# A two-level Winograd kernel: who makes the opening's block sums, where GpSimd waits, and the order of A12's products

## The chip, the cores and the metric

One NeuronCore of a Trainium2 chip. The metric is the device time of one execution in microseconds; a kernel's time is the median of its runs.

## The reference

With x of 1024 x 512, 64 weight matrices W_e of 512 x 512, and a linear layer with weights of 512 x 512 and a bias, all in float32:

```
out_lin     = x @ lin_w.T + lin_b
xv          = einsum('bf,efm->bem', x, weight)
zp          = einsum('bf,efm->bem', square(x), square(weight))
interaction = 0.5 * sum(square(xv) - zp, axis=1)
return out_lin + interaction
```

The sum over e of zp is one product, square(x) times the sum of the squared weights. What costs time is xv: 64 products of 1024 x 512 by 512 x 512.

## The kernel before, in words

**Tiling.** Four weight matrices side by side make one right-hand matrix B of 512 x 2048; 16 such groups ("quarters", q = 0 to 15) make up the 64. A is x. A times B is computed with Winograd's form of Strassen's method, on two levels, so that 7 x 7 = 49 block products stand in for 64. Each block product contracts over 128, has 256 rows (two halves j of 128) and 512 columns. Its left operand is a block sum of x, held in SBUF in `xs[:, outer, inner]`; its right operand is a block sum of the weights.

Blocks and sums are named by digits, on both levels alike. For x: "1" is A11, "2" is A12, "4" is A22, and "5" = A21 + A22, "6" = "5" - A11, "7" = A11 - A21, "3" = A12 - "6". A21 itself is not an operand. `outer_x(i)` (L154) makes the outer sum i in two instructions, one of 128x768 and one of 128x256. `inner_x(i)` (L178) makes the four inner sums of outer block i, in the order 5, 6, 7, 3 (L181 to L184), each 128x256. `a21_a22_sums` (L240, the sums themselves at L252) makes the inner sums of A21 and A22, which the linear layer needs. `xs` is made once, in the opening, and used by all quarters.

For the weights GpSimd makes the sums in every quarter: `outer_t` (L382) the outer ones, in place in the weight buffers or in T5 and T6, and `inner_t` the inner ones, `tp` (128x1024, L393), `t6` and `t4` (128x512, L395 and L397).

**A unit.** `unit(q, i, j)` is one outer product i and row half j: seven inner products on TensorE (L423) in the order 1, 5, 6, 2, 7, 3, 4 into three PSUM banks x, v and y. ScalarE copies x to y after product 1 (L477). VectorE adds the banks to earlier results in SBUF (L448 to L469), with ScalarE helping in unit 1. In a quarter the outer products come in the order 1, 2, 6, 7, 5, 3, 4. In unit 5 GpSimd also adds two halves of z with `rest` (L474). Results z are squared by ScalarE and added to `acc` by DMAs with accumulation that GpSimd issues (`gather`, L508). The squared weights are summed in `w2_sum` in the same way (L517 on ScalarE, L524 the DMA).

**The linear layer** stands ahead of quarter 0. `lin` (L204) multiplies A11 plainly (L214), ScalarE puts twice the result into acc (L224). A12's products are seven inner products of `lin_p` (L272, r = 0), those of A21 and A22 seven double ones (r = 1), into the banks x_lin, v_lin and y_lin. VectorE's `lin_add` (L315) and ScalarE's `twice` (L304) put the banks into acc or into the scratch s_lin. Each product that comes back to a bank has to wait until the last reader of that bank is through.

**What sets the order.** Nothing is scheduled by a planner: each step is put into a list with `st.at(t, fn)`, sorted by t, and issued in this order, and each engine keeps its own order. One unit of t is about one product; quarter q begins at 98 q. So the numbers t in the code decide what stands before what on each engine, and an engine that waits holds all that is queued behind it. The stretch that matters here is t = -30 to 1. Its block sums of x are placed at the end of the set-up code (L589 to L601), the linear layer's products by a loop (L327 to L344), and the weight sums of quarter 0 by the tables at L544 to L562. The order in the opening of the kernel before:

- VectorE: the inner sums of A11 and A12; the sums of A21 and A22 with L315 for A12 between them; the outer sums 5 and 6; L315 of A21/A22 for products 7 and 3; the inner sums of 6 and of 5.
- GpSimd: the sums of the linear weights (L285 to L293); one sum of A22 (L252); tp, t6, t4 of unit 1; both halves of T5; tp, t6, t4 of unit 2; the outer sums of 7 (L172) and its four inner sums; both halves of T6; the first w2_sum DMA; then the sums of unit 6.
- TensorE: A12's products in the order 1, 5, 6, 2, 7, 3, 4; then those of A21/A22 in the same order; then the units.

Of the kernel before, what the change touches and what calls it, by code (L numbers as in the profile page):

```python
# [28 lines left out]
def kernel(  # L29
# [31 lines left out]
    nc = tc.nc  # L61
# [45 lines left out]
    def xsl(i, o):  # L107
        return xs[:, SLOT[i], SLOT[o], :]

    st = Stream()  # L110
# [8 lines left out]
    a21 = {i: raw_sb[:, n, :] for n, i in enumerate("124")}  # L119
# [26 lines left out]
    def quarter(r, kk, n):  # L146

        w = slice(0, 3) if n is None else n
        for i, rk in BLOCK.items():
            if rk == (r, kk):  # L150
                return a21[i] if n == 3 else xs[:, SLOT[i], w, :]
        return A21[:, w, :]

    def outer_x(i, eng=nc.vector):  # L154
        if i in BLOCK:
            return []

        def put(n):
            w = slice(0, 3) if n is None else n

            def of(o):
                return a21[o] if n == 3 else xs[:, SLOT[o], w, :]

            def src(r, kk):
                return quarter(r, kk, n)

            if i == "5":
                eng.tensor_add(of(i), src(1, 0), src(1, 1))  # L168
            elif i == "6":
                eng.tensor_sub(of(i), of("5"), src(0, 0))  # L170
            elif i == "7":
                eng.tensor_sub(of(i), src(0, 0), src(1, 0))  # L172
            else:
                eng.tensor_sub(of(i), src(0, 1), of("6"))

        return [lambda: put(None), lambda: put(3)]

    def inner_x(i, eng=nc.vector):  # L178
        add, sub = eng.tensor_add, eng.tensor_sub
        return [  # L180
            lambda: add(xsl(i, "5"), a21[i], xsl(i, "4")),  # L181
            lambda: sub(xsl(i, "6"), xsl(i, "5"), xsl(i, "1")),
            lambda: sub(xsl(i, "7"), xsl(i, "1"), a21[i]),
            lambda: sub(xsl(i, "3"), xsl(i, "2"), xsl(i, "6")),  # L184
        ]

# [47 lines left out]
        return A21[:, SLOT[o]] if o in "124" else A21_SUMS[:, "5673".index(o)]  # L236

    def a21_a22_sums():  # L240
        def put(kk, o, eng):
            def of(o):
                return lin_x(kk, o)

            raw = a21["4"] if kk else A21[:, 3]
            fn, a, b = {
                "5": lambda: (eng.tensor_add, raw, of("4")),
                "6": lambda: (eng.tensor_sub, of("5"), of("1")),
                "7": lambda: (eng.tensor_sub, of("1"), raw),
                "3": lambda: (eng.tensor_sub, of("2"), of("6")),  # L250
            }[o]()
            fn(of(o), a, b)  # L252

        return [
            lambda o=o, kk=kk: put(kk, o, nc.gpsimd if o == "3" and kk else nc.vector)
            for o in "5673"
            for kk in range(2)
        ]

    def lin_p(r, o, bank, first):  # L260
        def fn():
            if o == "1":
                for n in "xvy":
                    LIN[r, n] = psum.tile(
                        [P, BK], F32, tag=n, name=f"{n}_lin{r}", bufs=2 if n == "x" else 3
                    )
                s_lin = spool.tile([P, 2, BK], F32, tag="s", name=f"s_lin{r}")
                LIN[r, "s2"], LIN[r, "s5"] = s_lin[:, 0], s_lin[:, 1]
            kks = range(2) if r else (1,)
            for kk in kks:  # L270
                for j in range(2):
                    nc.tensor.matmul(  # L272
                        LIN[r, bank][:, ts(j, HM)],
                        lin_x(kk, o, r)[:, ts(j, P)],
                        lin_rhs(lw_sb[:, ts(kk, 2)], LT[kk], o),
                        start=(first and kk == kks[0] and j == 0),
                        stop=True,
                        skip_group_check=True,
                    )

        return fn
# [19 lines left out]
    def twice(bank, dst):  # L301
        def fn():
            o = acc_blk(1, dst) if isinstance(dst, int) else by_j(LIN[1, dst])
            nc.scalar.activation(o, by_j(LIN[1, bank]), AF.Copy, scale=2.0)  # L304

        return fn

    def lin_add(r, bank, addend, dst):


        def of(n):
            return acc_blk(r, n) if isinstance(n, int) else by_j(LIN[r, n])

        def fn():
            nc.vector.scalar_tensor_tensor(  # L315
                of(dst), by_j(LIN[r, bank]), 2.0, of(addend), ALU.mult, ALU.add
            )

        return fn
# [4 lines left out]
        st.at(-30 + kk, lambda kk=kk: lin_t(LT[kk], lw_sb[:, ts(kk, 2)]))  # L324
    for n in range(4):
        st.at(-29 + 0.1 * n, lambda n=n: lin_out(n))
    for r, t0, dt in ((0, -21.5, 1), (1, -14, 2)):  # L327

        def copy_y(r=r):
            nc.scalar.copy(LIN[r, "y"], LIN[r, "x"])  # L330

        for n, (o, bank, first, fn) in enumerate(
            (
                ("1", "x", True, copy_y),
                ("5", "v", True, twice("v", "s5") if r else lin_add(0, "v", 3, "s5")),
                ("6", "y", False, twice("y", "s2") if r else lin_add(0, "y", 1, "s2")),
                ("2", "x", False, twice("x", 0) if r else lin_add(0, "x", 0, 0)),
                ("7", "y", False, lin_add(r, "y", "s5", 3)),
                ("3", "v", False, lin_add(r, "v", "s2", 1)),
                ("4", "y", False, twice("y", 2) if r else lin_add(0, "y", 2, 2)),  # L340
            )
        ):
            st.at(t0 + dt * n, lin_p(r, o, bank, first))
            st.at(t0 + dt * n + 0.25 * dt, fn)  # L344

    bias = const.tile([P, M], F32, tag="bias", name="bias")

# [189 lines left out]
    for q in range(NQ):  # L537
        g0 = 98 * q
        last = q == NQ - 1
        for kk, v, t in ((1, 0, -41), (0, 0, -37.5), (0, 1, -37), (1, 1, -3)):  # L540
            if q:
                st.at(g0 + t, lambda q=q, kk=kk, v=v: load_w(q, kk, v))

        for i, t0, t1 in (  # L544
            ("5", -9.9, 2) if q else ("5", -11, -10.9),
            ("6", 14.2, 14.3) if q else ("6", 0.5, 0.6),
            ("7", 28.7, 28.8),
            ("4", 50, 53),
        ):
            for u, t in enumerate((t0, t1)):  # L550
                st.at(g0 + t, lambda i=i, u=u: outer_t(i, u))
        for i, *times in (
            ("1", -6.4, -1.4, 2.1) if q else ("1", -11.5, -11.4, -11.3),
            ("2", 6.4, 6.5, 10.2) if q else ("2", -5, -4.9, -4.8),
            ("6", 20.7, 20.8, 27),
            ("7", 34.4, 34.5, 39.7),
            ("5", 43.1, 43.2, 43.3),
            ("3", 57.9, 58, 61.7),
            ("4", 81, 82.1, 84.1),
        ):  # L560
            for n, t in zip(("tp", "t6", "t4"), times):
                st.at(g0 + t, lambda q=q, i=i, n=n: inner_t(q, i, n))  # L562
        for n, (i, (addend, dst)) in enumerate(UNITS.items()):
            for j in range(2):
                unit(g0 + 14 * n + 7 * j, q, i, j, addend, dst)

        for k, n, r, times in (
            (1, "c", 0, ((None, 38.8), (None, 52.9))),
            (4, "c", 1, ((0, 73), (0, 84), (1, 80), (1, 91.5))),
            (5, "a", 0, ((0, 88), (0, 103.5), (1, 96.5), (1, 110.3))),  # L570
            (6, "b", 1, ((None, 111.3), (None, 124.2))),
        ):
            for j in range(2):
                t = g0 + 14 * k + 7 * j + 14.6
                squares(t - (0.95 if last and n == "b" else 0), q, n, j, 4 * (k == 4))
            for m, (j, t) in enumerate(times):
                if not last or n == "c":
                    gather(g0 + t, q, n, r, j, m % 2)
        if q == 0:
            w_times = (-6, 14.8, 37, 56.6)  # L580
        else:
            w_times = (-19.2, 14.8, 37, 56.6)
        for n, t in enumerate(w_times):
            w_squares(g0 + t, q, n // 2, n % 2)
    for kk, v in ((0, 0), (1, 0), (0, 1), (1, 1)):
        st.at(-100, lambda kk=kk, v=v: load_w(0, kk, v))


    for sums, *times in (  # L589
        (inner_x("1"), -29),  # L590
        (inner_x("2"), -22),
        (a21_a22_sums(), -21, -19.5, -18.5, -16.5, -15.5, -15),
        (outer_x("5") + outer_x("6"), -14.5),
        (inner_x("6") + inner_x("5"), -3.4),
    ):
        for n, fn in enumerate(sums):
            k = min(n, len(times) - 1)
            st.at(times[k] + 0.1 * (n - k), fn)
    for i, t in (("7", -4.7), ("3", 36.9)):
        for n, fn in enumerate(outer_x(i, nc.gpsimd) + inner_x(i, nc.gpsimd)):  # L600
            st.at(t + 0.1 * n, fn)  # L601

# [230 lines left out]
```

## Time and profile before

| | before |
|---|---|
| time of three runs, us | 1413.18, 1413.19, 1413.85 (median 1413.19) |
| the profiled execution: its own time / span, us | 1413.42 / 1411.6 |
| TensorE (PE) busy, us (share of the span) | 1403.0 (99%) |
| GpSimd (POOL) | 1257.2 (89%) |
| VectorE (DVE) | 879.9 (62%) |
| ScalarE (ACT) | 621.4 (44%) |
| start of the first product of the main loop (L423), us | 36.77 |
| weight blocks of quarter 0, four of 1 MB: issued, us | 6.08 and after |
| their landing after the issue, us (least, median, most) | 8.8, 11.3, 13.4 |

The profile is one execution. Times count from the start of the span. A line of the timeline has start, duration, engine, line of the code, operation, and output <- input by tile names with buffer numbers left out; "x4" counts records, and a TensorE instruction of this kernel leaves two. A bracket at the end is idle time of that engine before the line, and what ended it. [...] the pitch of the starts, not the duration, is a product's cost. A list of waits has the us in total, how often, and the longest.

### The profile page before, as it was taken

To read this page: it belongs to the slowest core of one execution; us is meant where nothing else is said; L and a number is where in the kernel's file an instruction comes from. 1 tells how busy PE (TensorE), PEld (TensorE's weight loads), DVE (VectorE), ACT (ScalarE), POOL (GpSimd) and SP (SyncE) were. 2 spreads that over 40 slices of the span, in tenths; PEclk is the share of its full clock that TensorE was granted. 3 is DMA by queue.
4 is the path that set the end of the run, shared out by engine and by line. 5 is a ranking of instruction groups with operands and counts; after the bars stand their busy time and mean duration, and the time that the engine had idled before them with its cause. 6 is when DMAs were issued, how large, how long until landed. Compare 5 with 4: busy or idle time off the path is not lost.

```text
span 1411.6 us, 11203 instructions
## 1 busy us (share of the span) xinstructions
PE 1403.0 (99%) x3352; PEld 640.5 (45%) x3352; DVE 879.9 (62%) x1269; ACT 621.4 (44%) x826; POOL 1257.2 (89%) x816
## 2 busy tenths in 40 slices
PE   8999999999999999999999999999999999999999
PEld 5444444444444444444444444444444444444446
DVE  7665665656566565666656566565656656566565
ACT  2435354443534534353443534444353453535443
POOL 6889899998999989899898988989899898989984
PEclk9999999999999999999999999999999999999999
DMA  5199899898989899898999989989898999989975
GB/s 216 30 221 206 176 225 181 205 215 191 201 176 227 178 220 203 189 215 168 215 202 216 197 170 229 182 202 213 194 205 172 222 188 218 201 179 223 182 165 134
DMA packets 58109, 273.63 MB, mean 194 GB/s; under 512 B 5441, under 2 KB 8001, under 8 KB 41793
## 3 DMA queue, kind: packets, MB, share of 16 engines
q0 software_dynamic: 36432, 198.20, 71.7%
q1 hardware_dynamic: 21328, 74.19, 15.0%
q10 hardware_dynamic: 288, 0.52, 0.1%
q8 instruction: 27, 0.44, 0.1%
q14 instruction: 34, 0.27, 0.0%
HBM read 72.61 MB, written 2.10 MB: 53 GB/s over the span
## 4 chain that ended last, share of the span: by engine, by line
PE 95%; POOL 2%; DVE 1%; DMA 1%; issue 1%; POOLq 0%; ACTq 0%; ACT 0%; DVEq 0%
PE y L423 40%; PE x L423 27%; PE v L423 27%; DMA acc<-z 1%; PE lin L214 1%; PE y_lin L272 0%; POOL z L474 0%; POOL acc L508 0%; DMA t<-lin_wT 0%; POOL w_sb L652 0%; DVE z L170 0%; DVE z L168 0%; POOL tp L393 0%; POOL w L632 0%; POOL t L636 0%
## 5 line engine op out<-in xcount | busy, mean ns | idle before, releaser
L423 PE MATMUL y<-t,xs 128*128 128x512 f32 x896 | 421.4, 593 | 0.0
L477 ACT COPY y<-x 128x512 f32<-128x512 f32 x224 | 127.7, 570 | 611.9 <-PE x L423 611.9
L469 DVE TENSOR_TENSOR z<-y,s 128x512 f32<-128x512 f32 x192 | 132.9, 692 | 244.6 <-PE y L423 244.6
L423 PEld LDWEIGHTS y<-t,xs 128*128 128x128 f32 x896 | 170.8, 191 | 213.4 <-issue 210.9
L499 ACT ACTIVATE z<-z 128x1024 f32<-128x1024 f32 x256 | 260.2, 1054 | 11.7 <-POOL z L474 9.2
L423 PE MATMUL x<-w,xs 128*128 128x512 f32 x512 | 249.4, 594 | 0.0
L423 PE MATMUL v<-tp,xs 128*128 128x512 f32 x448 | 229.2, 593 | 0.0
L423 PE MATMUL y<-tp,xs 128*128 128x512 f32 x448 | 228.9, 593 | 0.0
L508 POOL DMA_DIRECT2D acc<-z x190 | 213.1, 1152 | 15.2 <-DMA acc<-z 10.5
L393 POOL TENSOR_TENSOR tp<-w 128x1024 f32<-128x1024 f32 x64 | 175.6, 2744 | 23.8 <-PE y L423 22.5
L423 PE MATMUL x<-t,xs 128*128 128x512 f32 x384 | 188.4, 593 | 0.0
L474 POOL TENSOR_TENSOR z<-z,s 128x1024 f32<-128x1024 f32 x64 | 149.7, 2357 | 42.5 <-DVE s L469 42.5
L469 DVE TENSOR_TENSOR z<-v,s 128x512 f32<-128x512 f32 x192 | 132.8, 692 | 73.4 <-PE v L423 71.8
L460 DVE TENSOR_TENSOR z<-y,z 128x512 f32<-128x512 f32 x192 | 132.5, 690 | 57.2 <-PE y L423 57.2
L382 POOL TENSOR_TENSOR t<-w,t 128x1024 f32<-128x1024 f32 x64 | 164.4, 2731 | 0.0
L460 DVE TENSOR_TENSOR z<-x,z 128x512 f32<-128x512 f32 x192 | 132.4, 689 | 36.6 <-PE x L423 35.0
L423 PEld LDWEIGHTS x<-w,xs 128*128 128x128 f32 x512 | 97.9, 191 | 121.9 <-issue 120.7
L393 POOL TENSOR_TENSOR tp<-t 128x1024 f32<-128x1024 f32 x48 | 130.0, 2708 | 18.9 <-PE y L423 18.8
L423 PEld LDWEIGHTS v<-tp,xs 128*128 128x128 f32 x448 | 85.7, 191 | 107.4 <-issue 103.3
L423 PEld LDWEIGHTS y<-tp,xs 128*128 128x128 f32 x448 | 85.4, 191 | 106.4 <-issue 106.1
L423 PE MATMUL v<-w,xs 128*128 128x512 f32 x256 | 130.8, 593 | 0.0
L448 DVE TENSOR_TENSOR s<-v,z 128x512 f32<-128x512 f32 x160 | 110.7, 692 | 29.1 <-PE v L423 28.5
(118 smaller groups left out, 1491.3 us busy)
## 6 DMA issues: line engine op xcount, KB each, us to landing
w<-weight SPq DMA_DIRECT2D x64, 1024.0 KB, 13.4
acc<-z POOLq DMA_DIRECT2D x128, 512.0 KB, 8.4
w_sum<-w_sb POOLq DMA_DIRECT2D x63, 1024.0 KB, 9.3
acc<-z POOLq DMA_DIRECT2D x62, 1024.0 KB, 8.1
w<-x SPq DMA_DIRECT2D x2, 1024.0 KB, 8.3
out<-z SPq DMA_DIRECT2D x7, 256.0 KB, 2.3
xs<-x SPq DMA_DIRECT2D x2, 384.0 KB, 6.8
t<-lin_wT ACTq DMA_DIRECT2D x2, 256.0 KB, 4.2
```

Source lines behind the costliest of these rows:

```text
L214: nc.tensor.matmul(LIN[n], quarter(0, 0, (0, 1, 3, 2)[2 * s + l])[:, ts(j, P)], lw_sb[:, l, :], start=(l == 0), stop=(l == 1),)
L382: nc.gpsimd.tensor_sub(OUTER[i][:, u], a[:, u], b[:, u])
L393: nc.gpsimd.tensor_sub(t, b[:, 1], b[:, :, 0])
L423: nc.tensor.matmul(d[bank], xsl(i, o)[:, ts(j, P)], operand_b(q, i, o), start=start, stop=True, skip_group_check=True,)
L448: nc.vector.tensor_add(o, d[bank], zblk(q, addend, j, b))
L460: nc.vector.tensor_add(zblk(q, dst, j, b), d[bank], zblk(q, addend, j, b))
L469: nc.vector.tensor_add(s if both else zblk(q, dst, j, b), d[bank], s)
L474: nc.gpsimd.tensor_add(place(q, n)[:, 1, j], place(q, src)[:, 1, j], d["s"])
L477: st.at(t0 + 0.5, lambda: nc.scalar.copy(d["y"], d["x"]))
L499: lambda u=u: nc.scalar.activation(z[:, u, j], z[:, u, j], AF.Square),
L508: nc.gpsimd.dma_start(o, z, accum_op=ALU.add)
```

## The change

1. `inner_x` takes the sums to be made and their order as an argument.
2. In `a21_a22_sums` all eight sums are VectorE's; before, the sum "3" of A22 was GpSimd's.
3. The outer sums of 7 go from GpSimd to VectorE, and so do two of its inner sums, "7" and "5"; "6" and "3" stay with GpSimd, but stand far earlier in its order: "6" right after tp of unit 1, and "3" after t4 of unit 1. "6" needs "5", which is the last of VectorE's sums in the opening.
4. The inner sums of 5 go from VectorE to GpSimd, to t = 27.2, after the sums of unit 6.
5. On GpSimd the tp of unit 1 comes ahead of everything but the linear weights' sums; T5 comes after the sums of unit 2 and right ahead of T6.
6. A12's products come in the order 1, 5, 6, 2, 3, 7, 4, with the first product of A21/A22 ahead of the 4. Those of A21/A22 keep their order.
7. VectorE's order in the opening is then: inner sums of A11 and A12; L315 and the sums of A21/A22 mixed; the outer sums 5 and 6; the inner sums of 6; the outer sums of 7; L315 of A21/A22 on product 7; the inner sums "7" and "5" of 7; L315 on product 3.

ScalarE's and SyncE's orders stay as they are.

```diff
-    def inner_x(i, eng=nc.vector):
+    def inner_x(i, eng=nc.vector, which="5673"):
         add, sub = eng.tensor_add, eng.tensor_sub
...
+        return [fns[o] for o in which]
...
         return [
-            lambda o=o, kk=kk: put(kk, o, nc.gpsimd if o == "3" and kk else nc.vector)
+            lambda o=o, kk=kk: put(kk, o)
             for o in "5673"
             for kk in range(2)
         ]
...
-    for r, t0, dt in ((0, -21.5, 1), (1, -14, 2)):
...
-            st.at(t0 + dt * n, lin_p(r, o, bank, first))
-            st.at(t0 + dt * n + 0.25 * dt, fn)
+    def lin_unit(r, times):
...
+        for o, t in times.items():
+            bank, first, fn = work[o]
+            st.at(t, lin_p(r, o, bank, first))
+            st.at(t + 0.25, fn)
+    lin_unit(0, dict(zip("1562374", (-21.5, -20.5, -19.5, -18.5, -17.5, -16.5, -13.9))))
+    lin_unit(1, dict(zip("1562734", range(-14, 0, 2))))
...
-            ("5", -9.9, 2) if q else ("5", -11, -10.9),
+            ("5", -9.9, 2) if q else ("5", -4.3, -4.2),
...
-            ("1", -6.4, -1.4, 2.1) if q else ("1", -11.5, -11.4, -11.3),
-            ("2", 6.4, 6.5, 10.2) if q else ("2", -5, -4.9, -4.8),
+            ("1", -6.4, -1.4, 2.1) if q else ("1", -16, -4.9, -4.8),
+            ("2", 6.4, 6.5, 10.2) if q else ("2", -4.6, -4.5, -4.4),
...
-        (a21_a22_sums(), -21, -19.5, -18.5, -16.5, -15.5, -15),
-        (outer_x("5") + outer_x("6"), -14.5),
-        (inner_x("6") + inner_x("5"), -3.4),
+        (a21_a22_sums(), -21, -19, -18, -16.9, -15.9),
+        (outer_x("5") + outer_x("6") + inner_x("6"), -13.5),
+        (outer_x("7"), -6),
+        (inner_x("7", which="75"), -5.4),
+        (inner_x("7", nc.gpsimd, "6"), -5),
+        (inner_x("7", nc.gpsimd, "3"), -4.7),
+        (inner_x("5", nc.gpsimd), 27.2),
+        (outer_x("3", nc.gpsimd) + inner_x("3", nc.gpsimd), 36.9),
     ):
...
-    for i, t in (("7", -4.7), ("3", 36.9)):
-        for n, fn in enumerate(outer_x(i, nc.gpsimd) + inner_x(i, nc.gpsimd)):
-            st.at(t + 0.1 * n, fn)
```

More of the change, by code (lines that the diff above doesn't have):

```diff
@@ L176, in outer_x @@
         return [lambda: put(None), lambda: put(3)]
-    def inner_x(i, eng=nc.vector):
+    def inner_x(i, eng=nc.vector, which="5673"):
         add, sub = eng.tensor_add, eng.tensor_sub
[L180 to L185, printed above, removed]
+        fns = {
+            "5": lambda: add(xsl(i, "5"), a21[i], xsl(i, "4")),
+            "6": lambda: sub(xsl(i, "6"), xsl(i, "5"), xsl(i, "1")),
+            "7": lambda: sub(xsl(i, "7"), xsl(i, "1"), a21[i]),
+            "3": lambda: sub(xsl(i, "3"), xsl(i, "2"), xsl(i, "6")),
+        }
+        return [fns[o] for o in which]
     A21_SUMS = flat(ZT[1], 1, 8)[:, 4:8]
@@ L240, in a21_a22_sums, with put @@
     def a21_a22_sums():
-        def put(kk, o, eng):
+        def put(kk, o):
             def of(o):
@@ L246, in put @@
             fn, a, b = {
[L247 to L250, printed above, removed]
+                "5": lambda: (nc.vector.tensor_add, raw, of("4")),
+                "6": lambda: (nc.vector.tensor_sub, of("5"), of("1")),
+                "7": lambda: (nc.vector.tensor_sub, of("1"), raw),
+                "3": lambda: (nc.vector.tensor_sub, of("2"), of("6")),
             }[o]()
@@ L326, with copy_y @@
         st.at(-29 + 0.1 * n, lambda n=n: lin_out(n))
-    for r, t0, dt in ((0, -21.5, 1), (1, -14, 2)):
-        def copy_y(r=r):
+    def lin_unit(r, times):
+        def copy_y():
             nc.scalar.copy(LIN[r, "y"], LIN[r, "x"])
[L332 to L342, printed above, removed]
-            st.at(t0 + dt * n, lin_p(r, o, bank, first))
-            st.at(t0 + dt * n + 0.25 * dt, fn)
+        work = {
+            "1": ("x", True, copy_y),
+            "5": ("v", True, twice("v", "s5") if r else lin_add(0, "v", 3, "s5")),
+            "6": ("y", False, twice("y", "s2") if r else lin_add(0, "y", 1, "s2")),
+            "2": ("x", False, twice("x", 0) if r else lin_add(0, "x", 0, 0)),
+            "7": ("y", False, lin_add(r, "y", "s5", 3)),
+            "3": ("v", False, lin_add(r, "v", "s2", 1)),
+            "4": ("y", False, twice("y", 2) if r else lin_add(0, "y", 2, 2)),
+        }
+        for o, t in times.items():
[4 more added lines that the diff above has]
+    lin_unit(1, dict(zip("1562734", range(-14, 0, 2))))
     bias = const.tile([P, M], F32, tag="bias", name="bias")
```

## The prediction

> **What bounds the kernel now.** I read the waits of TensorE first, then the shares of the chain that ended last, then the timeline of 0 to 60 us with all engines, then the table by stretches of time, which has the granted clock, and last the same timeline around 100 us. TensorE's whole list of waits has three lines (us in total, times, longest):
>
> ```profile
> PE y_lin L272 <- DVE acc L315: 4.3, 1, 4.3
> PE y_spin L202 <- PEq L824: 0.8, 1, 0.8
> PE lin L214 <- DMA t<-lin_wT: 0.2, 1, 0.2
> ```
>
> The chain that ended last says the same from the other side:
>
> ```profile
> PE 95%; POOL 2%; DVE 1%; DMA 1%; issue 1%; POOLq 0%; ACTq 0%; ACT 0%; DVEq 0%
> ```
>
> So TensorE sets the time, and it has one hole, in the opening. From about 40 to 1360 us it never waits. The timeline (start, duration, engine, line) shows how the hole comes about:
>
> ```profile
> 18.36 2.53 POOL L393 TENSOR_TENSOR tp<-w 128x1024 f32<-128x1024 f32 x1
> ...
> 19.21 1.97 DVE L252 TENSOR_TENSOR xs<-xs,z 128x256 f32<-128x256 f32 x1
> ...
> 20.97 1.34 POOL L395 TENSOR_TENSOR t<-w,tp 128x512 f32<-128x512 f32 x1
> 21.10 1.49 DVE L252 TENSOR_TENSOR z<-z 128x256 f32<-128x256 f32 x1
> ...
> 29.99 2.55 DVE L170 TENSOR_TENSOR z<-z 128x256 f32<-128x256 f32 x1
> 32.34 1.33 POOL L395 TENSOR_TENSOR t<-w,tp 128x512 f32<-128x512 f32 x1
> 32.47 0.68 DVE L315 SCALAR_TENSOR_TENSOR acc<-y_lin,s_lin 128x512 f32<-128x512 f32 x1
> ```
>
> A 128x256 sum on VectorE takes 0.41 us where GpSimd is idle (12.55, 12.89). Here it takes 1.5 to 2.5 us: 19.21 + 1.97 = 21.18 is 0.29 us after GpSimd's 18.36 + 2.53 = 20.89. From 19.21 to 32.47 VectorE makes six sums, one per GpSimd instruction. The addition L315 at 32.47 is queued behind them, and the last product of y_lin cannot start before it, since it writes the bank that L315 reads. TensorE is idle from 28.9 to 33.2. Its clock falls as well (columns: stretch, length, busy PE, PEld, DVE, ACT, POOL, granted clock, DMA share, GB/s):
>
> ```profile
> 30.00:32.00 2.00, 0.00 (x0) 0.00 (x0) 2.00 (x2) 0.00 (x0) 2.00 (x1) 1.00 0.00 0
> 32.00:34.00 2.00, 0.81 (x2) 0.72 (x3) 2.00 (x4) 0.00 (x0) 1.84 (x3) 0.53 0.00 0
> 34.00:36.00 2.00, 2.00 (x6) 1.55 (x6) 1.97 (x3) 0.00 (x0) 2.00 (x2) 0.50 0.00 0
> ```
>
> **What the hole costs.** At full clock a product of the main loop starts every 0.857 us (four records in 1.72). The products before the hole are done at 27.85 + 0.86 = 28.71. Without idle time or half clock, the two y_lin steps (1.72) and the first three products of L423 (2.57) would end at 33.0. The fourth product starts at 40.6. The hole costs 7.6 us: 4.5 idle, 3.1 at half clock.
>
> [...] the sums above end just after GpSimd's instruction, while L315, with one input in PSUM, takes 0.67 to 0.69 us beside GpSimd as without it. [...] The trace has 0.50 after 4.3 us of idleness, until about 38.5; no run here shows what a shorter pause does. [...]
>
> **The change, part by part.**
> 1. *GpSimd held.* Its order becomes: tp of unit 1, then one sum of x7 (L182), which needs VectorE's last sum of x7 (L181), then the rest. The first weight block is issued at 6.08 and lands 8.8 us later, at 14.9. So tp runs 14.95 to 17.35 (2.40, as at 62.02) and then GpSimd waits. Queued behind the waiting sum are t6 and t4 of unit 1, tp, t6, t4 of unit 2, both halves of T5 and T6 and the first w2_sum transfer, all of which TensorE or the sum of squares needs later.
> 2. *VectorE's first stretch.* L315 on v at 13.72 and on y at 14.66 are done as before. The next sum (L252, ready 15.27) meets tp and ends at 17.64. Then, undisturbed: L315 on x 0.60, a sum 0.34, L315 on v 0.60, a sum 0.34. L315 on y starts at 19.44 and ends at 20.12.
> 3. *A12's order 1562374.* v's product comes before y's product 7, and A21/A22's first product before product 4. TensorE is through these at about 18.7, then product 4 waits for that L315 until 20.2: a new pause of 1.5 us.
> 4. *The rest of the opening on TensorE.* Product 4 (0.86) and six double products (1.72 each) end at 20.2 + 0.86 + 10.3 = 31.4. VectorE must have the sums for them: four L252 (1.34), L315 (0.6), outer sums 5 and 6 (0.87 + 0.34 twice), inner sums of 6 (1.34), outer sums of 7 (1.21) from 20.1: done at 27.0. L315 on y's product 7 then waits for TensorE (28.0 and 0.17 more) and ends near 28.8, before product 4 of A21/A22 is due at 29.7. The old hole is gone. The first L423 product starts at 31.4 and the fourth at 34.0, against 40.6: **6.6 us earlier**.
> 5. *GpSimd's release.* L183 and L181 follow L315: GpSimd goes on at 29.45. Two sums (0.75 each), tp 2.45, t6 and t4 twice (1.35 + 1.25), T5 and T6 (4.7 each) add up to 18.5: 48.0. The old kernel reaches this place at 46.3, but then waits until 51.2 for squares that follow TensorE; now these are done by about 44.5. So the transfer is issued 3.2 us earlier than before. The four sums of x5, which move here from VectorE, cost 2.9. From there GpSimd is 0.3 us earlier than before, and 0.9 after a wait of 0.58 at 85.31 falls away, while TensorE is 6.6 earlier.
> 6. *What is late next.* Of the steps that GpSimd hands TensorE I compared ready and due. tp of unit 7: ready 64.4, due 73.05, slack 8.7, now 2.3. t4 of unit 7: 73.3 and 81.6, now 2.0. tp of unit 5: 76.5 and 85.07, now 2.2. All hold. The tightest is tp of unit 4:
>
> ```profile
> 99.85 4.68 POOL L474 TENSOR_TENSOR z<-z,s 128x1024 f32<-128x1024 f32 x2 [0.55 <-DVE s L469]
> ...
> 104.49 0.83 POOL L508 DMA_DIRECT2D acc<-z  x1
> ...
> 105.09 2.63 POOL L393 TENSOR_TENSOR tp<-t 128x1024 f32<-128x1024 f32 x1
> ...
> 109.10 1.02 PE L423 MATMUL v<-tp,xs 128*128 128x512 f32 x2
> ```
>
>    It was ready at 107.72 and due at 109.10. GpSimd's idle time before its two pairs of L474 (2.68 and 0.55) shrinks to nothing: it arrives at 90.25 instead of 91.15, and the tp is ready at 103.6. Due: 109.10 - 6.63 = 102.47. **TensorE waits 1.1 us.** Net gain 5.5. From quarter 2 on GpSimd's own idle time (42.5 us in 32 waits before L474, 41.3 in 30 before tp) takes up what is late, so nothing repeats.
> 7. ScalarE's and SyncE's instruction orders are unchanged; no DMA is added. GpSimd's w2_sum and acc transfers keep their order among themselves. Moving the x5 sums off VectorE is at nothing: VectorE is idle 1.46 us before L469 at 43.21 already.
>
> Sum: profiled execution 1413.42 (span 1411.6 and 1.8 around it) - 5.5 = 1407.9. The median of the runs is 0.2 lower, 1413.19: **1407.7 us**.
>
> **Bounds of the unknown.** The new pause is between 0 (GpSimd's tp does not collide) and 2.4 (a whole tp more); each microsecond goes one to one into GpSimd's release and the end. A weight block landing after 15.3 would let the first sum through and block the next, 0.3 better. If GpSimd's chain is 1.1 shorter than I sum, the wait at unit 4 is gone: gain 6.6. With neither pause nor that wait it is 8.
>
> **Rivals.**
> - *The hold costs nothing later* (gain 6.6 to 8, 1405.2 to 1406.6): for it speaks that each slack was over 8 us; against it the 1.38 us at unit 4. Chance 0.17.
> - *The new pause halves the clock.* [...] GpSimd's release moves with it: gain 2.1 to 3.8, 1409.4 to 1411.1. Against it: [...] the trace's one fall came after 4.3. Chance 0.13.
> - *The sums don't get ahead*: some other step holds VectorE, the old hole stays in part, and with half a hole and its cold clock the time is within 2.8 us of before, 1411 to 1415. Against it: every sum in the stretch has its inputs by 20 us. Chance 0.08.
> - *GpSimd becomes the bound (slower).* The wait at unit 4 comes back in each of the 16 quarters, 16 x 1.1 = 18, less 6.6: 1424. It decides if GpSimd's lateness exceeds the idle time before L474 in a quarter, about 2.7 us, i.e. if its release comes after about 31. Against it: the idle time is there in every quarter, and GpSimd is busy 89%. Chance 0.06.
>
> **Numbers.** Likeliest, as worked out, gain 4.6 to 6.4: chance 0.56. Range 1405.3 to 1410.6: it holds the likeliest case, nearly all of the first rival and over half of the second. A measurement of this kernel can tell about 0.2%, 2.8 us. Faster 0.82 (a third of the second rival falls short of 2.8), same 0.12, slower 0.06.
>
> **What would show it.** Right: no DVE acc L315 wait of 4.3 us; one of 1 to 2 us near 19 to 20; clock 1.00 from 30 to 40; GpSimd idle from 17.4 to about 29.4 on VectorE; first L423 product near 31.4; a wait of about 1 us on tp near 103. Wrong: half clock after 20 us, sums of VectorE still above 1 us between 18 and 27, TensorE waits on GpSimd in later quarters.

## The result and the profile after

| | before | changed |
|---|---|---|
| median of 22 runs each, us | 1413.12 | 1410.78 |
| lowest and highest, us | 1412.27, 1413.89 | 1409.78, 1412.15 |
| the profiled execution: its own time / span, us | 1413.42 / 1411.6 | 1412.15 / 1410.3 |

The ratio is 0.9984, with a 95% interval of 0.9977 to 0.9991. The kernel is faster by 2.3 us, a small gain that is clear of the noise. One run of the kernel "the same, and x5 on VectorE" in the table of experiments took 2507.72 us at a granted clock of 0.556 and is left out of that kernel's median. The forecast was 1407.7 with a range of 1405.3 to 1410.6: the direction was right, the gain of 5.5 was more than twice what came, and the median lies 0.2 above the range. The execution that was profiled is the slowest of the 22, so the sums below, which are of this execution, come out at a gain of 1.3 and not of 2.3.

The longest waits of TensorE in the changed kernel (us in total, times, longest; two of 0.2 us are left out):

```profile
PE y L427 <- ACT s L450: 2.3, 1, 2.3
PE y_lin L272 <- DVE acc L315: 1.5, 1, 1.5
PE y_spin L203 <- PEq L832: 0.8, 1, 0.8
```

The hole of 4.3 us is gone. The pause of 1.5 us that was forecast is there. The first line was not forecast: TensorE waits 2.3 us for a ScalarE copy, and no wait on a tp of GpSimd is in the list.

The opening goes nearly as forecast. The timeline of the changed kernel:

```profile
15.51 2.35 POOL L397 TENSOR_TENSOR tp<-w 128x1024 f32<-128x1024 f32 x1 [3.31 <-DMA w<-weight]
15.67 2.47 DVE L252 TENSOR_TENSOR xs<-z,xs 128x256 f32<-128x256 f32 x1
...
20.76 1.10 PE L272 MATMUL y_lin<-z,xs 128*128 128x256 f32 x4 [1.49 <-DVE acc L315]
...
22.50 0.95 DVE L168 TENSOR_TENSOR xs<-z,xs 128x768 f32<-128x768 f32 x1
...
30.31 0.73 POOL L182 TENSOR_TENSOR xs<-xs 128x256 f32<-128x256 f32 x1 [12.45 <-DVE xs L181]
...
32.06 1.02 PE L427 MATMUL x<-w,xs 128*128 128x512 f32 x2
...
34.76 1.88 PE L427 MATMUL x<-w,xs 128*128 128x512 f32 x4
```

GpSimd makes one tp, one VectorE sum runs into it (2.47 us instead of 0.41), then GpSimd is held for 12.45 us and the sums run undisturbed. The 128x768 sum takes 0.95 us. The first product of the main loop starts at 32.06, against 36.77 before, and the clock stays full. The fourth starts at 34.76; in the kernel before this was:

```profile
40.43 1.88 PE L423 MATMUL x<-w,xs 128*128 128x512 f32 x4
```

Then ScalarE, in the same kernel, from 78 us on:

```profile
78.74 0.57 ACT L481 COPY y<-x 128x512 f32<-128x512 f32 x1 [5.44 <-PE x L427]
84.00 2.00 ACT L521 ACTIVATE w_sb<-w 128x1024 f32<-128x1024 f32 x2 [4.69 <-DMA w_sum<-w_sb]
85.91 0.57 ACT L450 COPY s<-v 128x512 f32<-128x512 f32 x1
86.38 0.59 ACT L450 COPY s<-y 128x512 f32<-128x512 f32 x1
...
87.02 1.65 PE L427 MATMUL y<-tp,xs 128*128 128x512 f32 x2 [2.31 <-ACT s L450]
```

ScalarE is to square the fourth pair of weights of quarter 0 into w2_sb (L521; the profile calls the buffer w_sb), but that buffer is still read by GpSimd's transfer of the third pair into w2_sum. (This transfer is called the third here, after its pair. It is the second that GpSimd issues, since the first pair is squared straight into w2_sum.) ScalarE stands still for 4.69 us, and the copies of unit 5, which TensorE's product 7 needs, are queued behind it. The transfer itself is on time by the old clock. These are GpSimd's issue and, from the view of DMA issues, the time to its landing, in the kernel before and then in the changed one:

```profile
72.97 1.16 POOL L524 DMA_DIRECT2D w_sum<-w_sb  x1
...
w_sum<-w_sb POOLq DMA_DIRECT2D x1, 1024.0 KB, 10.2
```

```profile
71.22 0.85 POOL L512 DMA_DIRECT2D acc<-z  x1
71.82 1.54 POOL L401 TENSOR_TENSOR t<-w,t 128x512 f32<-128x512 f32 x1
73.04 1.17 POOL L528 DMA_DIRECT2D w_sum<-w_sb  x1
...
w_sum<-w_sb POOLq DMA_DIRECT2D x1, 1024.0 KB, 10.9
```

Its issue and its landing hardly move, while TensorE has come 5.7 us earlier. In the kernel before the squares began at 84.89, straight after ScalarE's copy:

```profile
84.41 0.57 ACT L477 COPY y<-x 128x512 f32<-128x512 f32 x1 [5.44 <-PE x L423]
84.89 2.01 ACT L517 ACTIVATE w_sb<-w 128x1024 f32<-128x1024 f32 x2
...
87.84 0.58 ACT L446 COPY s<-y 128x512 f32<-128x512 f32 x1 [0.47 <-PE y L423]
...
90.22 1.02 PE L423 MATMUL y<-tp,xs 128*128 128x512 f32 x2
```

The transfer had landed at about 72.97 + 10.2 = 83.2. That is a slack of 1.7 us for a step that TensorE was to run ahead of by more than 6. Between the squares and TensorE's product 7 there was a little more to spare: 0.47 us of idle time before the second copy, and 1.8 us from its end at 88.42 to the product at 90.22. All in all the chain had 4.0 us. TensorE came 5.67 us earlier and the transfer landed 0.8 later, at 83.9, so the product had to be 5.67 + 0.8 - 4.0 = 2.5 us late, which is what it was.

The pause of TensorE costs more than its length in this execution, as the table by stretches shows (length, busy PE, PEld, DVE, ACT, POOL, granted clock, DMA share, GB/s):

```profile
84.00:86.00 2.00, 0.71 (x2) 0.00 (x0) 1.18 (x2) 2.00 (x3) 2.00 (x2) 1.00 1.04 209
86.00:88.00 2.00, 0.98 (x2) 0.63 (x3) 0.00 (x0) 1.45 (x4) 1.92 (x2) 0.87 1.27 184
88.00:90.00 2.00, 2.00 (x3) 0.67 (x2) 0.69 (x1) 0.00 (x0) 2.00 (x3) 0.50 0.69 207
90.00:92.00 2.00, 2.00 (x5) 0.89 (x4) 0.34 (x1) 0.58 (x1) 0.55 (x1) 0.78 1.02 190
```

Where the gain went can be read off four places on TensorE, before less after, by the starts, since the records overlap (in the changed kernel the product at 36.48 is 1.02 long and the next starts at 37.34, 0.86 later): the fourth product of L423, 40.43 - 34.76 = 5.67 us; unit 5's product 7, right after the pause, 90.22 - 87.02 = 3.20; unit 4's tp product, after the half clock, 109.10 - 107.70 = 1.40; the last product, 1406.67 - 1405.44 = 1.23. The pause took 2.5, the half clock 1.8.

Not every execution seems to have the half clock. Of the changed kernel's 22 runs the ten with a mean granted clock of 1.000 took 1409.78 to 1410.98 us, the eight with 0.999, the profiled one among them, 1410.68 to 1412.15, and the four with 0.998 took 1411.30 to 1411.80. Only one of the 22 has a trace, so for the others this is read from the mean clock alone.

### The profile page after: what moved, and what is told of

Same layout as the page of the kernel before. It is cut to its first block, busy times and chain, and to the rows that moved or that the text cites. A ratio compares the mean times of both kernels' runs of the same rounds, so it can differ in the third digit from the quotient of the medians.

```text
span 1410.3 us, 11201 instructions
## 1 busy us (share of the span) xinstructions
PE 1402.1 (99%) x3352; PEld 637.6 (45%) x3352; DVE 867.2 (61%) x1270; ACT 621.3 (44%) x826; POOL 1252.2 (89%) x815
## 4 chain that ended last, share of the span: by engine, by line
PE 92%; POOL 4%; DMA 2%; issue 1%; DVE 0%; ACT 0%; POOLq 0%; ACTq 0%; DVEq 0%
PE y L427 39%; PE v L427 26%; PE x L427 26%; DMA acc<-z 1%; DMA w_sum<-w_sb 1%; POOL tp L397 1%; PE lin L215 1%; POOL t L386 0%; POOL t L401 0%; PE y_lin L272 0%; POOL t L399 0%; POOL acc L512 0%; POOL z L478 0%; POOL w L386 0%; DMA t<-lin_wT 0%
## 5 line engine op out<-in xcount | busy, mean ns | idle before, releaser
L503 ACT ACTIVATE z<-z 128x1024 f32<-128x1024 f32 x256 | 260.1, 1054 | 11.7 <-POOL z L478 9.2
L521 ACT ACTIVATE w_sb<-w 128x1024 f32<-128x1024 f32 x126 | 125.9, 1050 | 6.3 <-DMA w_sum<-w_sb 4.7
```

The lines of the kernel that those rows point to most:

```text
L503: lambda u=u: nc.scalar.activation(z[:, u, j], z[:, u, j], AF.Square),
L521: nc.scalar.activation(o, WB[kk][v][:, u], AF.Square)
```

## The experiments

All twelve kernels ran in up to five rounds beside the kernel before; each ratio is to the runs of before on the same chip (medians 1412.81 to 1413.28). They ran on four chips, so a difference of a few tenths of a microsecond between two medians of the table says little. The theory is called the ring theory in the expectations: GpSimd's transfer frees w2_sb, ScalarE's squares wait for it, ScalarE's copies stand behind the squares, TensorE waits for the copies. The main rivals: GpSimd's lateness in the weight sums takes the time, or only the opening counts.

| kernel | median, us | ratio to before (95%) |
|---|---|---|
| changed kernel | 1410.78 | 0.9984 (0.9977 to 0.9991) |
| transfer earlier | 1408.78 | 0.9969 (0.9957 to 0.9980) |
| squares later, load misplaced | 1420.95 | 1.0059 (1.0046 to 1.0071) |
| squares later, load behind them | 1408.71 | 0.9972 (0.9961 to 0.9983) |
| GpSimd not held | 1410.40 | 0.9982 (0.9975 to 0.9989) |
| additions first | 1410.30 | 0.9979 (0.9973 to 0.9986) |
| x5 sums back on VectorE | 1407.61 | 0.9962 (0.9950 to 0.9975) |
| A12's old order | 1411.88 | 0.9989 (0.9983 to 0.9996) |
| before, with A12's new order | 1413.23 | 1.0002 (0.9994 to 1.0010) |
| transfer earlier, additions first | 1407.50 | 0.9962 (0.9949 to 0.9976) |
| the same, and x5 on VectorE | 1406.91 | 0.9957 (0.9944 to 0.9971) |
| additions first, x5 on VectorE | 1406.71 | 0.9951 (0.9938 to 0.9963) |
| transfer, additions, x5, quarter 1's squares later | 1406.97 | 0.9954 (0.9940 to 0.9968) |

**Is it the ring? The transfer issued earlier.**

```diff
-                t + (3.2 if t < 0 else 5),
+                36.5 if t == 36 else t + (3.2 if t < 0 else 5),
...
-            w_times = (-6, 14.8, 37, 56.6)
+            w_times = (-6, 14.8, 36, 56.6)
```

The third pair of squares moves up by one step, and its transfer with it, ahead of the sums of x3.

> The changed kernel, with the third w2_sum transfer of quarter 0 issued ahead of the sums of x3 on GpSimd instead of behind them and behind t4 of unit 7. Ring theory: it is issued near 66 instead of 73, lands near 76, the squares no longer wait, and the time is the same as with the squares placed later, about 1408.5. Rival: 1410.8, with TensorE waiting elsewhere.

Measured: 1408.78. The transfer is issued at 65.51 and takes 7.0 us, and ScalarE's squares wait for nothing:

```profile
65.51 0.87 POOL L528 DMA_DIRECT2D w_sum<-w_sb  x1
...
78.93 2.01 ACT L521 ACTIVATE w_sb<-w 128x1024 f32<-128x1024 f32 x2
```

The wait on the ScalarE copies of unit 5 is gone, the clock is 1.00 throughout from 84 to 90, and what limits next is the step that the forecast had named. TensorE's longest waits (two of 0.2 us are left out):

```profile
PE y_lin L272 <- DVE acc L315: 1.4, 1, 1.4
PE y_spin L203 <- PEq L832: 0.8, 1, 0.8
PE v L427 <- POOL tp L397: 0.4, 1, 0.4
```

The ring theory holds; the rival fails. The two 95% intervals touch (0.9957 to 0.9980 against 0.9977 to 0.9991), but all six runs, at 1407.53 to 1409.38, lie below the fastest of the changed kernel's 22. TensorE waits 0.4 us for the tp of unit 4, where 1.1 was forecast.

**The same from the other end: ScalarE's squares later.** The first try moved the squares and the transfer that follows them:

```diff
-                t + (3.2 if t < 0 else 5),
+                t + (3.2 if t < 0 else 0.25 if t == 63.6 else 5),
...
-            w_times = (-6, 14.8, 37, 56.6)
+            w_times = (-6, 14.8, 37, 63.6)
```

> The changed kernel, with ScalarE's last pair of weight squares of quarter 0 placed behind unit 5's first copies instead of ahead of them (their transfer to w2_sum follows them). Ring theory: TensorE's 2.3 us wait near 85 us came from these squares, which wait for the third w2_sum transfer and hold ScalarE's copies of unit 5. Then the wait and the half clock after it are gone, and the time falls by 2 to 2.5, to about 1408.5, where tp of unit 4 becomes the next limit (a wait of about 1 us near 103). Rival (GpSimd's lateness itself takes the time): another wait takes its place and the time stays at 1410.8.

Measured: 1420.95, a miss. At 63.6 the squares stand behind the issue of quarter 1's load into the same block, which is at 61. So they wait for that load, and this kernel squares a slice of quarter 1's w01 in place of quarter 0's: it no longer computes the same sum, and its time is used for nothing but the wait. ScalarE's timeline:

```profile
84.07 0.57 ACT L481 COPY y<-x 128x512 f32<-128x512 f32 x1 [1.99 <-PE x L427]
98.92 2.00 ACT L521 ACTIVATE w_sb<-w 128x1024 f32<-128x1024 f32 x2 [14.29 <-DMA w<-weight]
```

TensorE waited 11.9 us for a copy behind them and then ran at half clock until about 105 (granted clock 0.50 from 102 to 104, 0.71 from 104 to 106). It says nothing against the ring, but shows what ScalarE's queue did to TensorE with this wait of 14.29 us at its head. The second try moved the load behind the squares:

```diff
+                late = (q, kk, v) == (1, 0, 1)
+                st.at(63.75 if late else g0 + t, lambda q=q, kk=kk, v=v: load_w(q, kk, v))
```

> The changed kernel with ScalarE's last pair of weight squares of quarter 0 behind unit 5's copies again, and this time the load of quarter 1's block w01 behind those squares too, so that they square quarter 0's weights. Ring theory: no wait of TensorE near 85 us, 1408.5 to 1409. Rival (the load that now starts later is missed by GpSimd near 110 us): TensorE waits there and the time is 1410 or more.

Measured: 1408.71, the same as with the earlier transfer. TensorE no longer waits near 85 us. Two edits that have only the ring in common each give about 2 us. The later load is not missed by TensorE; GpSimd waits 0.98 us for a weight block at 110, and no wait of TensorE follows from it.

**What is the hold worth?**

```diff
-        (inner_x("7", nc.gpsimd, "6"), -5),
-        (inner_x("7", nc.gpsimd, "3"), -4.7),
+        (inner_x("7", nc.gpsimd, "6"), -4.35),
+        (inner_x("7", nc.gpsimd, "3"), -4.34),
```

> The changed kernel, with GpSimd's two sums of x7 placed behind t4 of unit 2, so that GpSimd is not held after its first tp but makes t6, t4, tp, t6, t4 beside VectorE's sums. [...] each of these five takes one VectorE sum with it; the first pause of TensorE grows to about 2.5, a second one of about 2.3 comes back before A21/A22's product 4, and the first product of the main loop starts near 35 instead of 32. But GpSimd is some 3 us earlier from there on, so the 2.3 us wait near 85 is gone too: the time is 1410 to 1411.5, as with the hold. Rival (the hold is worth its 3 us at the end as well): 1413 to 1414.

Measured: 1410.40, no different from the changed kernel. The first product of the main loop starts at 34.22, 2.2 us later than with the hold; TensorE's first pause is 2.29 us and is followed by half clock:

```profile
22.00:24.00 2.00, 2.00 (x6) 1.61 (x5) 2.00 (x2) 0.00 (x0) 1.84 (x3) 0.50 0.20 76
```

The second pause of 2.3 did not come. GpSimd had done five sums in the meantime, and ScalarE waited only 1.14 us for the third transfer, TensorE not at all. So the hold wins 2.2 us in the opening, and in the time nothing of it is left: with the hold the ring's wait is there, without it it is not.

**VectorE's additions ahead of the sums.**

```diff
-        (a21_a22_sums(), -21, -19, -18, -16.9, -15.9),
+        (a21_a22_sums(), -21, -16.2),
```

> The changed kernel, with VectorE's additions L315 of A12's products 2, 3 and 7 ahead of the sums of A21/A22 but the first. [...] no addition stands behind the sum that meets GpSimd's first tp, so TensorE's pause of 1.5 us is gone, and with it GpSimd's release and all that follows comes 1.5 earlier: 1409.3. Rival (what is won in the opening is lost at the wait near 85): that wait grows to 3.8 and the time stays at 1410.8.

Measured: 1410.30, between the two forecasts. The pause of 1.5 us is gone and the first product starts at 29.89, 2.2 us earlier. The wait at the ring grew, from 2.3 to 3.1:

```profile
PE y L427 <- ACT s L450: 3.1, 1, 3.1
PE y_spin L203 <- PEq L832: 0.8, 1, 0.8
PE lin L215 <- DMA t<-lin_wT: 0.2, 1, 0.2
```

GpSimd follows the opening and issues the third transfer 2.1 us earlier (70.90), but it takes 11.7 us and not 10.9, so that ScalarE's squares start only 1.4 earlier (82.64). That part of the expectation, that all would move together, was wrong. The medians differ by 0.5 us, less than their intervals tell apart.

**One part undone: the sums of x5 back on VectorE.**

```diff
-        (inner_x("5", nc.gpsimd), 27.2),
+        (inner_x("5"), -3.4),
```

> The changed kernel with the four inner sums of x5 back on VectorE, ahead of unit 1's additions as in the kernel before: one part of the change undone. Ring theory: GpSimd has 2.9 us of sums less [...] so the third w2_sum transfer is issued 1.5 to 1.7 earlier and lands earlier; TensorE's wait near 85 shrinks from 2.3 to about 0.7 and its clock stays full: 1408 to 1409. Rival (only the length of the opening counts): 1410.8, or later if the x5 sums delay VectorE.

Measured: 1407.61, better than either theory had it. The third transfer is issued at 70.20 instead of 73.04, 2.84 us earlier (the 1.5 to 1.7 of the expectation rested on an estimate of the author's that no trace shows), ScalarE waits 1.65 us instead of 4.69, and TensorE waits neither for ScalarE near 85 nor for the tp of unit 4:

```profile
80.46 2.00 ACT L521 ACTIVATE w_sb<-w 128x1024 f32<-128x1024 f32 x2 [1.65 <-DMA w_sum<-w_sb]
```

VectorE's four sums look expensive there, but they take little from GpSimd:

```profile
30.64 1.41 DVE L181 TENSOR_TENSOR xs<-z,xs 128x256 f32<-128x256 f32 x1
32.08 1.38 DVE L182 TENSOR_TENSOR xs<-xs 128x256 f32<-128x256 f32 x1
33.38 0.94 DVE L183 TENSOR_TENSOR xs<-xs,z 128x256 f32<-128x256 f32 x1
34.25 2.56 DVE L184 TENSOR_TENSOR xs<-xs 128x256 f32<-128x256 f32 x1
```

```profile
31.84 1.33 POOL L401 TENSOR_TENSOR t<-w,t 128x512 f32<-128x512 f32 x1
33.13 0.91 POOL L184 TENSOR_TENSOR xs<-xs 128x256 f32<-128x256 f32 x1
34.01 2.52 POOL L397 TENSOR_TENSOR tp<-w 128x1024 f32<-128x1024 f32 x1
36.61 1.33 POOL L399 TENSOR_TENSOR t<-w,tp 128x512 f32<-128x512 f32 x1
```

In the changed kernel the same four GpSimd instructions take 1.26, 0.72, 2.35 and 1.27. The sums cost GpSimd 0.5 us in all, and on GpSimd they took 2.9. The change's own step of moving them to GpSimd costs it about 3 us, more than its whole gain of 2.3; here the two intervals do not overlap.

**The other part: A12's order.** In the changed kernel, undone:

```diff
-    lin_unit(0, dict(zip("1562374", (-21.5, -20.5, -19.5, -18.5, -17.5, -16.5, -13.9))))
+    lin_unit(0, dict(zip("1562734", (-21.5, -20.5, -19.5, -18.5, -17.5, -16.5, -15.5))))
```

> The changed kernel with A12's products in the order 1, 5, 6, 2, 7, 3, 4 again, all ahead of A21/A22's first product: the other part of the change undone. [...] product 4 meets the same addition, which is as late, with 1.7 us of products less ahead of it: TensorE's pause grows from 1.5 to about 2.3, the first product of the main loop starts 0.6 later, and GpSimd's release with it: 1411.4. Rival (the order is worth nothing, since the wait near 85 takes up the difference): 1410.8. Rival (the order carries much of the change): 1413.

Measured: 1411.88. The pause is 1.92 us instead of 1.49, and the first product starts at 32.31, 0.25 later and not 0.6. The difference of 1.1 to the changed kernel is nearly twice what was expected, and the two intervals overlap. In this trace TensorE also waits 0.6 us near 108 for a ScalarE copy, which the changed kernel does not; so how much the order itself is worth stays open. The pause at the ring is 2.25 us long here, and the clock stays full after it:

```profile
88.00:90.00 2.00, 2.00 (x6) 0.88 (x5) 0.69 (x1) 0.59 (x1) 2.00 (x3) 1.00 0.65 158
```

And alone, in the kernel before:

```diff
+            t = t0 + dt * n if r or o not in "734" else {"7": -16.5, "3": -17.5, "4": -13.9}[o]
+            st.at(t, lin_p(r, o, bank, first))
+            st.at(t + 0.25 * dt, fn)
```

> The kernel before with nothing changed but A12's order (1, 5, 6, 2, 3, 7, 4, with A21/A22's first product ahead of the 4). [...] the hole of 4.3 us is set by VectorE's sums beside GpSimd and stays; the addition for product 4 now stands behind the slow sums too and puts 0.6 on top: 1413 to 1413.8. Rival (the order alone brings the gain): 1411 to 1412.

Measured: 1413.23, ratio 1.0002: nothing. The hole is 5.2 us long and ends where it did. So the order alone does not bring the gain.

**Both cures together, and with x5.**

> The changed kernel with both edits that each alone gave something: the third w2_sum transfer ahead of the sums of x3, and VectorE's additions ahead of the sums of A21/A22. Ring theory: with the ring open, all of the 2 us that the additions win in the opening arrive at the end: 1406.5 to 1407.3. Rival (another limit stands right behind): as with the transfer alone, 1408.8.

Measured: 1407.50, just above what the ring theory gave. With the ring open, the additions seem to be worth 1.3 us over the transfer alone (1.0 by the ratios), where they were worth 0.5 with it closed; the intervals overlap in both cases, so this is not shown.

> As the run before, and the inner sums of x5 on VectorE. Ring theory: GpSimd's lateness at tp of unit 4 (a TensorE wait of 0.4 us there with the earlier transfer) is gone too: 0.4 to 0.8 below the run before, 1406 to 1406.8. Rival (quarter 1's weight loads or accumulating transfers are the next limit): no gain over the run before, with GpSimd waiting on DMA near 110 to 122.

Measured: 1406.91. The gain of 0.6 has the right size but lies within both intervals. The wait on the tp of unit 4 is gone; TensorE now waits 0.9 us near 104 for a ScalarE copy behind squares that wait for a weight load of quarter 1. So the rival was right in part: a next limit stands close behind.

> The changed kernel with VectorE's additions ahead of the sums of A21/A22 and the inner sums of x5 back on VectorE, and the third w2_sum transfer where the change has it. Ring theory: TensorE is 1.7 us ahead of the run with x5 alone, and there ScalarE's copies had 0.8 us to spare after the transfer; so a wait of 0.4 or less comes back near 82, and a second of about 0.9 near 104, where ScalarE's squares wait for quarter 1's weight loads: 1406.5 to 1407.2. Rival (the opening's gain goes to the end): 1405.8.

Measured: 1406.71, the lowest of all, though not told apart from the kernels near it. It is 6.6 us under the kernel before on the same chip, and its interval lies below that of the changed kernel. The ring is back with 0.8 us, where 0.4 or less was expected, and the second wait did not come.

The last run moves quarter 1's first squares behind a copy:

```diff
-            w_times = (-19.2, 14.8, 37, 56.6)
+            w_times = (-13.3 if q == 1 else -19.2, 14.8, 37, 56.6)
```

> The best so far (transfer earlier, additions first, x5 on VectorE), and ScalarE's first pair of weight squares of quarter 1 behind the copy of unit 4's first half instead of ahead of it. The run without this had one wait of TensorE left, 0.9 us near 104, on a ScalarE copy behind these squares, which waited for a weight load. If that was it, the wait is gone and the time falls by 0.9 to about 1406.1; if GpSimd's T5 of quarter 1 waits for the same loads and passes it on, there is no gain: 1407.

Measured: 1406.97, no gain. TensorE's wait near 104 is gone. GpSimd waits 1.02 us for a weight block at 108 and TensorE 0.2 for a tp at 114.5. That is the second of the two ways expected; whether those 0.2 us and the differences of the opening from run to run account for all of it stays open.

## Why the prediction was wrong, step by step

- **Hold and first stretch (steps 1 and 2)**: right. tp ran from 15.51 to 17.86 (forecast 14.95 to 17.35; the weight block landed 0.6 later), and the sum that meets it ends 0.28 us after it.
- **The new pause (step 3)**: right, 1.49 us against 1.5, at full clock (1.00 in every stretch from 12 to 42 us). That the number is so exact is luck: tp and the linear layer were both late, by 0.6 and 0.4 us. In other runs with the same opening the pause was 0.65 (the misplaced load), 1.15 (x5 on VectorE) and 1.44 us (the transfer earlier).
- **The rest of the opening (step 4)**: right in its mechanism, 0.9 us too large in its gain. The first product starts at 32.06 against 31.4, the fourth at 34.76 against 34.0, about half of the difference because the linear layer began 0.4 us later in this execution (12.12 against 11.72). The 0.87 us a 128x768 sum that this step reckons with was the author's estimate; from the start of such a sum to the next start it is 0.86 to 0.87 here (22.50 to 23.37, 23.71 to 24.57, 26.50 to 27.37). The gain of 6.6 was too large by another 0.2: the old start of 40.6 was read from the chain, where the timeline has 40.43.
- **GpSimd's release and chain (step 5)**: right, to within 0.9 us. GpSimd went on at 30.31 against 29.45, the first transfer at 48.49 against 48.0, the x5 sums 54.50 to 57.37, 2.9. From there on GpSimd was to be 0.3 us earlier than before; it was 0.07 later (73.04 against 72.97).
- **"What is late next" (step 6)**: this step failed. The prediction wrote that "of the steps that GpSimd hands TensorE I compared ready and due", and compared only the tp, t6 and t4. GpSimd hands on one more thing, the end of its transfer out of w2_sb, and by way of ScalarE. Its slack was 1.7 us at ScalarE and 4.0 at TensorE, less than all but one of those compared. The prediction had even named "the first w2_sum transfer" as queued behind the held sum, and then took the later ones as harmless because they "keep their order among themselves" (step 7). Order was kept; time against TensorE was not. It cost 2.5 us, and 1.8 more by the clock in the profiled execution. With the ring opened, by either of two edits, the time is 1408.7 to 1408.8, inside the range.
- **tp of unit 4**: the wait of 1.1 us did not come, because TensorE was late at this place already, by the ring. With the ring open it is there, at 0.4 us. The place was right, the size too large.
- **"Moving the x5 sums off VectorE is at nothing"**: true for VectorE, but it was the wrong side to look at. Their 2.9 us on GpSimd were in the sum of step 5. That they stood ahead of the one transfer with little slack was not seen.
- **The sum**, for the profiled execution: the gain of 5.5 lacks 0.9 of the opening, 2.5 of the pause and 1.8 of the half clock, and is spared the 1.1 of unit 4. That leaves 1.4; 1.27 was measured (1413.42 - 1412.15).
- **The rivals**: half clock after a pause came, but at a pause that no rival had. The gain left to the second rival rests on an estimate of the author's for how long the clock stays low; in the traces the half clock cost 3.1 us after the 4.3 us hole of the kernel before and 1.8 after the pause of 2.3. "The hold costs nothing later" fell; "GpSimd becomes the bound" fell too: after quarter 0 nothing repeats, and the only wait of TensorE that stands later in the list is one of 0.2 us ahead of the last products.

## What to carry to other kernels

When the bounding engine is to be moved ahead, list all that it meets, also over two engines. For each wait of the old trace that was just met (a transfer that landed shortly before its buffer was written again), the slack is due less landed; add to it the idle time on each engine between there and the bounding one. The smallest of these sums caps what the bounding engine keeps at that place: here 4.0 us, less the 0.8 by which the transfer landed later, and TensorE kept 3.2. Look for these where an engine shows no idle time at all before an instruction with a wait, as ScalarE did here at 84.89. And work given to an engine that is not the bound may still stand in front of the one thing that others need from it.

## What the hardware showed that was not expected

- In the run with the x5 sums on VectorE, VectorE's and GpSimd's sums delayed each other, but not at equal cost: VectorE's four 128x256 sums took 0.94 to 2.56 us instead of 0.41, each ending 0.28 to 0.29 us after a GpSimd instruction, while four GpSimd instructions were only 0.06 to 0.19 us longer than in the changed kernel.
- A pause of TensorE of 2.3 us was followed by half clock in two traces and not in a third: the clock was 0.50 at 88 to 90 us in the changed kernel's profile, 0.50 at 22 to 24 us after the 2.29 us without the hold, and 1.00 throughout 84 to 92 after a pause of 2.25 us in the run with A12's old order. What decides between the two is not shown here.
- The third transfer, 1 MB from GpSimd's queue, took 10.2 us (before) to 11.7 us (additions first) with an acc transfer issued 1.8 us ahead of it, and 7.0 us where no other transfer of GpSimd was issued within 6 us (the run with the transfer earlier).
